# A graph layer with a 32-expert feed-forward on one core: smaller expert blocks, four rounds in place of three, and another way of handing out work beside the edge loop

## The chip, the cores and the metric

The kernel runs on one core of a Trainium2 chip. The metric is the device time of one execution in microseconds, given as the median of several runs; lower is better. Besides the timed runs there is one execution recorded by the hardware profiler, and all durations below come from that one.

## The reference

Only what matters here is kept. There are 6250 nodes with 256 features and 106,250 directed edges (sorted by target) with 64 features each.

```python
xn = layernorm(x)
# 1. edges: gather the source's features, project, SiLU, sum by target, layer norm
msgs = silu(concat(xn[src], edge_attr) @ W + b)            # 106250 x 320 @ 320 x 256
gnn  = layernorm(segment_sum(msgs, dst, 6250)) * gamma + beta
# 2. linear attention: 8 heads of 64, k and v normalised per head
dots = einsum('nhd,nhe->hde', k, v)
attn = einsum('nhd,hde->nhe', q, dots) / 6250 @ Wout.T + bout
x = x + gnn + attn
# 3. top-1 routing to 32 experts, each 256 -> 64 -> 256
xf  = layernorm(x); idx = argmax(xf @ router_w.T + router_b)
h   = relu(xf @ W1[idx] + b1[idx])
out = x + relu(h @ W2[idx] + b2[idx])
```

## The kernel before

Nodes lie in 49 tiles of 128 rows (the last has 106), X holding the running sum and `wide` the transposed normalised rows, later the rows that go to the experts. All arithmetic is f32. The program has three parts.

**The preamble** loads x, normalises it, multiplies it by W's upper part and writes the product to `proj` in DRAM, so that an edge only has to gather a finished 256-row. It also checks that the edges are sorted as assumed (`flag`), and a branch on all engines then takes either `ordered`, the normal path, or `general`, a slow one that works for any edges.

**The edge loop** in `ordered` goes over 208 groups of 512 edges. Per group GpSimd (POOL) issues four indirect gathers of 128 rows (L1213), three groups ahead; TensorE (PE) turns the edge features (`turn`, L1229) and multiplies them (L1356); VectorE (DVE) adds the gathered rows (L1360) and makes a selection matrix (L1366); ScalarE (ACT) applies SiLU (L1377); and every second group PE sums messages by target in two levels (`level1` L1308, `level2` L1335). A gather buffer is free again only after `level1`, so POOL can be at most about three groups ahead of PE. The instruction order is the program's own: the whole of `ordered` is written under a manual schedule, and each engine works through its list in order.

**Everything else** is handed out beside the loop by `Work`: pieces are generators that yield a nominal PE time, DVE time and delay, and `Work.step` runs once per group and takes pieces until an allowance (2.7 us of PE, 3.8 us of DVE, more in one group of two) is spent. The pieces are the attention (`attention_batch`, two tiles at a time, L468 to L503), then for each chunk of tiles whose sums are closed the routing (`chunk`), and then the experts in three rounds of 24, 16 and 9 tiles. A round gives each token a row (`slot`), sends the tokens with indirect writes into the DRAM tensor `xs` (`send`, L854; popped from a list in `gather`, at most two after every second gather), computes expert blocks of 128 rows two at a time (`experts`, `layers`), writes them to `ys`, and reads the results back by token (`collect`, `fetch`, L1024). A block's two weight matrices come from a table in DRAM (`wtab`) that the kernel itself builds (`tabulate`): SyncE (SP) reads the expert's number into a register (L937) and issues one load (L938). The last round is different (`own`): it has one block for each expert, so all weights are loaded in advance by ACT's queue (`own_weights`, after the loop), and the bias is added when the result is read back (L1041 to L1045).

When the loop is over, `Work.drain` runs what is left without an allowance. All 49 read-backs lie there, since `collect` waits for the pool `last` that is opened only then. At the very end a second branch looks at `over`: if a round had too few blocks, the experts are computed again (`again`).

Of the kernel before, what the change touches and what calls it, by code (L numbers as in the profile page):

```python
# [31 lines left out]
CHUNKS = (6, 6, 6, 6, 6, 5, 5, 5, 4)  # L32
CH = max(CHUNKS)
FIRST = (3, 6, 10, 10, 10, 10)
AB = 2
BB = 2
LEAD = 3
AHEAD = 4
BESIDE = 2
ALLOWANCE = (2.7, 3.8)  # L40


ROUNDS = ((24, 44), (16, 38), (9, None))
# [11 lines left out]
def kernel(  # L55
# [167 lines left out]
    counting = const.tile([P, 3, P], BF16, name="counting")  # L223
    nc.vector.tensor_copy(counting[:, 2, :], ident)
# [18 lines left out]
    row_of = const.tile([P, NQ], F32, name="row_of")  # L243
    flag = const.tile([1, 1], I32, name="flag")
# [31 lines left out]
    with tc.tile_pool(name="prep", bufs=2) as prep, tc.tile_pool(name="pre_ps", bufs=2, space=PSUM) as pre_ps:  # L276
# [88 lines left out]
        nc.vector.tensor_copy(flag, pb)  # L365
# [43 lines left out]
    WROW = DC * HID + D  # L409
    wtab = dram.tile([NE, P, WROW], F32, name="wtab")  # L410

    def tabulate(engine, e0, e1):
        q = slice(e0, e1)
        a = DC * HID
        engine.dma_start(
            wtab[q, :, :a].rearrange("e p w -> (e p) w"), w1[q, :, :].rearrange("e (p c) h -> (e p) (c h)", c=DC)
        )
        for i in range(BB):
            engine.dma_start(wtab[q, i * HID : (i + 1) * HID, a:], w2[q, :, :])

# [3 lines left out]
    def weights(pool, bank, w):  # L424
# [3 lines left out]
        w.update(kv_w=kv_w, dots=dots)  # L428
        nf = 2 * F // P
        raw = pool.tile([P, nf, D], F32, tag="kv", name="raw", bufs=2)  # L430
        nc.sync.dma_start(raw, wqkv[F:, :].rearrange("(f p) c -> p f c", p=P))
# [3 lines left out]
        yield 0.0, 0.0, 1  # L435
        for f in range(0, nf, 2):
            pt = bank("t", [P, DC, 2, P], "pt")
            for c in range(DC):
                for i in range(2):
                    nc.tensor.transpose(pt[:, c, i, :], raw[:, f + i, c * P : (c + 1) * P], ident)  # L440
            nc.scalar.copy(kv_w[:, :, f * P : (f + 2) * P], pt.rearrange("p c i e -> p c (i e)"))
            yield 0.5, 0.0, 0
# [15 lines left out]
    def attention_batch(pool, bank, w, t0, t1):  # L458
# [3 lines left out]
        kv = pool.tile([P, AB, 2, F], F32, name="kv", bufs=2)  # L462
        var = small.tile([P, AB * 2 * HEADS], F32, name="var")
        for j in range(m):
            for s in range(2):
                b = bank("kv", [P, F], f"kv{s}")
                for c in range(DC):
                    nc.tensor.matmul(  # L468
                        b, xnT(t0 + j, c), kv_w[:, c, s * F : (s + 1) * F], start=(c == 0), stop=(c == DC - 1)
                    )  # L470
                nc.scalar.copy(kv[:, j, s, :], b)
                yield 1.9, 0.0, 1
            sq = pool.tile([P, 2 * HEADS, DH], F32, name="sq")
            nc.scalar.activation(sq, kv[:, j].rearrange("p s (h d) -> p (s h) d", d=DH), AF.Square)  # L474
# [4 lines left out]
        yield 0.0, 0.0, 1  # L479
# [5 lines left out]
        yield 0.0, 2.4, 1  # L485
        for j in range(m):
            k = kv[:, j, 0, :].rearrange("p (h d) -> p h d", d=DH)
# [3 lines left out]
        for h in range(HP):  # L491
            for j in range(m):
                for i in range(2):
# [3 lines left out]
                        kv[:, j, 0, q],  # L497
                        kv[:, j, 1, q],
# [4 lines left out]
        nc.vector.tensor_add(dots, pd, dots)  # L503
        yield 0.6 * m, 0.4, 0

    def attention_matrix(pool, bank, w):

        raw = pool.tile([P, 2, HP, D], F32, tag="kv", name="raw", bufs=2)
        wq, rawo = raw[:, 0], raw[:, 1].rearrange("p h c -> p (h c)")
# [4 lines left out]
        made = pool.tile([P, 2, HP, D], F32, tag="kv", name="made", bufs=2)  # L514
        qd, wo_t = made[:, 0], made[:, 1]
        diag = pool.tile([P, HP, P], F32, tag="sq", name="diag")
        nc.vector.memset(diag, 0.0)
        yield 0.0, 0.2, 1
# [24 lines left out]
    class Nodes:  # L543


        def __init__(self, pool, bank, rounds, in_order):
# [10 lines left out]
            self.so_far = pool.tile([P, BB, NE], F32, name="so_far")  # L557
# [4 lines left out]
            most = (N + (P - 1) * NE) // P + BB  # L562
            self.number = pool.tile([BB * NE, most], F32, name="number")
# [7 lines left out]

            self.upto = pool.tile([BB * NE, BB * NE], F32, name="upto")
            self.b2_sb = pool.tile([BB * NE, D], F32, name="b2_sb")
            nc.vector.memset(self.upto, 0.0)
            for i in range(BB):
                q = slice(i * NE, (i + 1) * NE)
                nc.vector.tensor_add(self.upto[q, q], after[q, q], ident[q, q])
                nc.sync.dma_start(self.b2_sb[q, :], b2)
# [24 lines left out]
            self.at = {}  # L603

        def clear(self, r, b0, b1):
            nc.sync.dma_start(
                r.xs[b0 * P : b1 * P, :].rearrange("(b p) d -> p b d", p=P),
                zero[:, None, :].to_broadcast([P, b1 - b0, D]),
# [24 lines left out]

        def chunk(self, t0, t1):
# [11 lines left out]
            for t in range(t0, t1):  # L646
                p = self.bank("kv", [P, D], "pres")
                for c in range(DC):
                    nc.tensor.matmul(p, xnT(t, c), mix[:, c, :], start=(c == 0), stop=(c == DC - 1))
                nc.vector.tensor_add(X[:, t, :], p, X[:, t, :])  # L650
                moments(mv2, t - t0, X[:, t, :])
                yield 0.9, 1.0, 0
            self.at[t0] = 1
            yield 0.0, 0.0, 1
# [3 lines left out]
            yield 0.0, 2.2, 1  # L658
# [64 lines left out]
            nc.tensor.matmul(pr[:, 1, 0, :], ones[0:1, :], self.so_far[0:1, 0, :], start=True, stop=True)  # L723
# [9 lines left out]
            nc.vector.tensor_copy(self.so_far, ahead[:, None, :, m].to_broadcast([P, BB, NE]))  # L733
            nc.vector.tensor_mul(logit, logit, hot)
            nc.vector.tensor_reduce(self.rank[:, t0:t1], logit, axis=AX.X, op=ALU.add)
            yield 1.2, 2.2, 1
            self.at[t0] = 3
            if r.own:
                row = small.tile([P, CH], F32, name="place")
                nc.vector.scalar_tensor_tensor(  # L740
                    row[:, :m], top[:, :m], float(-P), self.rank[:, t0:t1], op0=ALU.mult, op1=ALU.add
                )
                nc.vector.tensor_scalar_add(row[:, :m], row[:, :m], float(NE * P))
                self.within(r, t0, t1, row, self.rank[:, t0:t1], P)
                if t1 == r.t1:
                    most = small.tile([1, 1], F32, name="most")
                    nc.vector.tensor_reduce(most, self.so_far[0:1, 0, :], axis=AX.X, op=ALU.max)
                    self.count(most, P)
# [5 lines left out]
        def within(self, r, t0, t1, row, what, limit):  # L754
# [6 lines left out]
                float((r.nb - r.t0) * P),  # L761
# [8 lines left out]
            nc.vector.tensor_scalar_min(self.back[:, t0:t1], self.slot[:, t0:t1], float(r.nb * P - 1))  # L770
# [6 lines left out]
        def places(self, pool, r):  # L777
# [3 lines left out]
            def to_blocks(p, shape, name):  # L781
                i = pool.tile(shape, I32, name=f"{name}_i", bufs=1)
                nc.vector.tensor_scalar_add(i, p, float(P - 1))
                nc.vector.tensor_scalar(i, i, 7, None, op0=ALU.logical_shift_right)
# [4 lines left out]
            both = BB * NE  # L789
            pe = self.bank("kv", [both, 1], "pcount")  # L790
            counts = self.so_far[0:1, :, :].rearrange("o i e -> o (i e)")
            nc.tensor.matmul(pe, counts, ones[0:1, 0:1], start=True, stop=True)
            blocks = to_blocks(self.so_far[:, 0, :], [P, NE], "blocks")
# [4 lines left out]
            column = to_blocks(pe, [both, 1], "column")  # L798
            for c0, c1 in chunks:
                if not t0 <= c0 < t1:  # L800
# [10 lines left out]
                    row[:, :m], first[:, :m], float(P), self.rank[:, c0:c1], op0=ALU.mult, op1=ALU.add  # L811
                )
                self.within(r, c0, c1, row, row[:, :m], nb * P)
# [3 lines left out]
            pe = self.bank("kv", [both, 1], "pends")  # L817
            nc.tensor.matmul(pe, self.upto, column, start=True, stop=True)
            ends = pool.tile([both, 2], F32, name="ends", bufs=1)
# [3 lines left out]
            passed = pool.tile([both, nb], F32, name=f"passed{r.name}", bufs=1)  # L823
            nc.vector.tensor_scalar(passed, number, ends[:, 1:2], None, op0=ALU.is_ge)
            chosen = pool.tile([both, nb], F32, name=f"chosen{r.name}", bufs=1)
# [5 lines left out]
            nc.tensor.matmul(px, ones[:NE, 0:1], passed[:NE, :], start=True, stop=True)  # L831
# [728 lines left out]
    with path.Else():  # L1560
        general()
# [45 lines left out]
```

## Time and profile before

| what | value |
|---|---|
| median of 3 runs | 1425.09 us (1419.56 to 1426.43) |
| profiled execution | 1422.18 us, span 1420.5 us |
| PE, DVE, ACT, POOL busy | 1118.7, 851.6, 541.2, 939.6 us |
| mean granted TensorE clock | 0.877 of full speed |
| DMA | 245.16 MB, mean 173 GB/s |
| first gather issued / last one | 104.0 us / 1217.5 us |

The span is what the profiler recorded from first to last event; the 1.7 us between it and the execution's own time lie around it. Busy times overlap, and idle time of an engine costs nothing unless another waits for it. PE is busy for the largest share, but its share is an average over stages with different limits.

### The profile page before, as it was taken

What the parts mean: (1) busy time and instruction counts of PE and PEld (TensorE: products, weight loads), DVE (VectorE), ACT (ScalarE), POOL (GpSimd) and SP (SyncE); (2) the same over time, 40 slices, a digit from 0 to 9 for tenths busy, and PEclk for the clock granted to TensorE, in tenths of its full rate; (3) what the DMA queues carried; (4) which work ended last, traced back from release to release, by engine and by line L of the source; (5) the groups of instructions that cost most, each with busy time, mean ns of one, the idle gap of its engine ahead of it and who ended that gap; (6) DMA issues with size and microseconds to landing.
All of it is one profiled execution on the core that took longest, in us unless ns stands there. A gap on an engine that the chain in (4) does not pass through costs nothing.

```text
span 1420.5 us, 22703 instructions
## 1 busy us (share of the span) xinstructions
PE 1118.7 (79%) x7340; PEld 656.5 (46%) x7340; DVE 851.6 (60%) x2256; ACT 541.2 (38%) x987; POOL 939.6 (66%) x1050
## 2 busy tenths in 40 slices
PE   4876898899988888988987875489889766857862
PEld 3653444445444444545654543255555433534440
DVE  6933766767766676677876773256556644435342
ACT  2543555455445444543333332134344322212120
POOL 3537777777777777777777777777777677316222
PEclk9997999999999999999999877599999797866585
DMA  7238777655555554445444444478887546589672
GB/s 242 78 107 234 203 198 213 198 172 168 160 156 169 159 170 131 130 131 164 133 127 134 132 119 121 143 203 243 250 241 217 139 118 191 160 244 282 210 242 71
DMA packets 251813, 245.16 MB, mean 173 GB/s; under 512 B 130176, under 2 KB 221736, under 8 KB 251676
## 3 DMA queue, kind: packets, MB, share of 16 engines
q0 software_dynamic: 44960, 121.67, 29.3%
q1 hardware_dynamic: 196152, 113.91, 27.3%
q10 hardware_dynamic: 10564, 7.95, 1.9%
q8 instruction: 63, 1.03, 0.3%
q14 instruction: 74, 0.61, 0.2%
HBM read 194.34 MB, written 55.38 MB: 176 GB/s over the span
## 4 chain that ended last, share of the span: by engine, by line


## 5 line engine op out<-in xcount | busy, mean ns | idle before, releaser
L1213 POOL DMA_INDIRECT gat<-proj,src_T x831 | 796.8, 959 | 266.4 <-issue 219.8
L1360 DVE TENSOR_TENSOR gat<-h,gat 128x1024 f32<-128x1024 f32 x208 | 254.1, 1222 | 280.2 <-PE h L1356 148.0
L1377 ACT ACTIVATE gat<-gat 128x1024 f32<-128x1024 f32 x208 | 219.8, 1057 | 242.9 <-DVE gat L1360 205.8
L1356 PE MATMUL h<-ge,eT 64*128 64x256 f32 x1664 | 251.6, 423 | 33.2 <-DVE gat L1360 32.3
L1356 PEld LDWEIGHTS h<-ge,eT 64*128 64x128 f32 x1664 | 155.0, 198 | 137.1 <-issue 98.8
L1335 PE MATMUL sum<-part,s 128*128 128x256 f32 x400 | 129.6, 452 | 93.3 <-DVE s L1324 93.0
L468 PE MATMUL kv<-kv_w,wide 128*128 128x512 f32 x392 | 188.0, 606 | 3.2 <-DVE kv_w L450 3.2
L1233 ACT COPY eT<-pt 128x256 f32<-128x256 f32 x208 | 77.3, 371 | 204.6 <-PE pt L1229 195.0
L1335 PEld LDWEIGHTS sum<-part,s 128*128 128x128 f32 x400 | 78.7, 215 | 144.8 <-DVE s L1324 129.0
L1308 PE MATMUL po<-gat,s 128*32 128x256 f32 x1664 | 130.8, 439 | 0.0
L1024 POOL DMA_INDIRECT ot<-yso,back x49 | 48.5, 990 | 101.3 <-DVE wide L688 28.0
L1317 ACT COPY part<-po 128x256 f32<-128x256 f32 x104 | 38.7, 372 | 187.2 <-PE po L1308 187.2
L1229 PE MATMUL pt<-ident,ea 128*128 128x128 f32 x416 | 93.7, 308 | 2.2 <-DMA ea<-in_edge_attr_dram 1.4
L468 PEld LDWEIGHTS kv<-kv_w,wide 128*128 128x128 f32 x392 | 68.4, 193 | 57.5 <-issue 52.3
L475 DVE TENSOR_REDUCE var<-sq 128x16 f32<-128x1024 f32 x49 | 59.7, 1218 | 52.1 <-ACT sq L474 52.0
L896 DVE COPY xbT<-pt 128x512 f32<-128x512 f32 x57 | 39.2, 688 | 73.9 <-PE pt L894 73.7
L1308 PEld LDWEIGHTS po<-gat,s 128*32 128x32 f32 x1664 | 47.8, 121 | 67.7 <-issue 35.8
L1229 PEld LDWEIGHTS pt<-ident,ea 128*128 128x128 f32 x416 | 42.8, 144 | 75.2 <-issue 50.0
L854 POOL DMA_INDIRECT xso<-wide,slot x49 | 49.3, 1006 | 27.1 <-DVE back L770 16.7
L299 POOL TENSOR_TENSOR X<-X,bo 128x256 f32<-128x256 f32 x49 | 35.5, 746 | 47.7 <-ACT xn L296 25.9
L894 PE MATMUL pt<-ident,xb 128*128 128x128 f32 x228 | 49.2, 349 | 21.6 <-DMA xb<-xso 19.9
L306 PE MATMUL pp<-gw,wide 128*128 128x256 f32 (+1 forms) x196 | 53.5, 417 | 13.8 <-ACT wide L303 6.6
(264 smaller groups left out, 1391.7 us busy)
## 6 DMA issues: line engine op xcount, KB each, us to landing
ea<-in_edge_attr_dram SPq DMA_DIRECT2D x207, 128.0 KB
xb<-xso SPq DMA_DIRECT2D x57, 256.0 KB
xso<-zero SPq DMA_DIRECT2D x28, 512.0 KB
wt<-wtab SPq DMA_DIRECT2D x72, 192.0 KB
gat<-proj,src_T POOLq DMA_INDIRECT x831
yso<-xb SPq DMA_DIRECT2D x41, 256.0 KB
wtab<-in_L_ffn_W_dram SPq DMA_DIRECT2D x24, 256.0 KB
out_dram<-ot SPq DMA_DIRECT2D x48, 128.0 KB
```

The costliest lines, as they stand in the source:

```text
L306: nc.tensor.matmul(pp[:n, :], xnT(t, c, n), gw[:, c, :], start=(c == 0), stop=(c == DC - 1))
L468: nc.tensor.matmul(b, xnT(t0 + j, c), kv_w[:, c, s * F : (s + 1) * F], start=(c == 0), stop=(c == DC - 1))
L475: nc.vector.tensor_reduce(var[:, j * 2 * HEADS : (j + 1) * 2 * HEADS], sq, axis=AX.X, op=ALU.add)
L854: ins = nc.gpsimd.indirect_dma_start(out=r.xs[:], out_offset=bass.IndirectOffsetOnAxis(ap=self.slot[:n, t : t + 1], axis=0), in_=wide[:n, ...
L1213: nc.gpsimd.indirect_dma_start(out=gat[:n, k % 2, k // 2, :], out_offset=None, in_=proj[:], in_offset=bass.IndirectOffsetOnAxis(ap=src_T[: ...
L1229: nc.tensor.transpose(pt[:, j, :], ea[:, 2 * j : 2 * j + 2, :].rearrange("p k d -> p (k d)"), ident)
L1233: nc.scalar.copy(eT, pt)
L1308: nc.tensor.matmul(po[k * wide_k : (k + 1) * wide_k, :], s1[:, k, :], msg[:, k % 2, k // 2, :], start=(g == here[0]), stop=(g == here[-1]) ...
L1335: nc.tensor.matmul(sums[t], s2[:, (t - lo) * P : (t - lo + 1) * P], part, start=(q == opens[t]), stop=(q == closes[t]),)
L1356: nc.tensor.matmul(h[:, s, j, :], eTs[g][half, j, :], ge[half, :], start=True, stop=True)
L1360: nc.vector.tensor_add(gats[g], h, gats[g])
L1377: nc.scalar.activation(gats[g], gats[g], AF.Silu)
```

## The change

Six things change together.

1. Expert blocks have 64 rows (HB) and are computed four at a time, a "quad" of 256 rows, where before there were pairs of 128. In `layers` the bias product comes first, and each half of an output tile belongs to another expert.
2. The rounds are 28, 11, 5 and 5 tiles; the last two are `own` rounds with one 64-row block per expert. The last chunks are 3 and 2 tiles.
3. The table `wtab` is gone. A quad loads W1 and W2 of its four experts straight from the inputs (eight loads, four register reads). The `own` weights go into the places of `wide` whose tokens have been sent, during the loop, on SP's queue; read-backs use places of `wide` too. The own rounds add their bias on PE, as the others do.
4. `Work.step` runs twice a group, before and after SiLU and the sums, with half the allowance each, and up to 1.5 us not spent is carried over. Attention may have three batches in flight in place of two, with smaller buffers; the products with `mix` of later tiles are made as soon as `mix` is known.
5. The last groups' sums are written out behind the loop, which has 208 iterations in place of 212; the last chunks are urgent.
6. The branch at the start and `again` are gone: `ordered` always runs, and one branch at the end runs `general` if either check failed.

```diff
-CHUNKS = (6, 6, 6, 6, 6, 5, 5, 5, 4)
+CHUNKS = (6, 6, 5, 5, 6, 6, 5, 5, 3, 2)
+HB = 64
+QB = 2 * BB
-ALLOWANCE = (2.7, 3.8)
-ROUNDS = ((24, 44), (16, 38), (9, None))
+ALLOWANCE = (((1.9, 2.0), (1.9, 2.0)), ((1.3, 1.8), (0.3, 1.8)))
+CARRY = 1.5
+ROUNDS = ((28, 76), (11, 44), (5, None), (5, None))
+BACK = (32, 44)
...
+            for j in pairs:
+                for i in range(BB):
+                    nc.tensor.matmul(py[j][i * HB : (i + 1) * HB, :], one_of(BB * j + i).to_broadcast([NE, HB]),
+                        self.b2_sb, start=True, stop=False, tile_position=(0, i * HB))
+            for j in pairs:
+                for i in range(BB):
+                    half = slice(i * HID, (i + 1) * HID)
+                    nc.tensor.matmul(py[j][i * HB : (i + 1) * HB, :], hid[half, j, :], w2_of(BB * j + i, half),
+                        start=False, stop=True, tile_position=(i * HID, i * HB))
...
         def experts(self, pool, r, b0):
-                last = queue.dma_start(w[:, i, :], wtab[bass.ds(e, 1), :, :].rearrange("o p w -> p (o w)"))
+                queue.dma_start(wa[:, b : b + 1, :], w1[bass.ds(e, 1), :, :].rearrange("o (p c) h -> p o (c h)", c=DC))
+                last = queue.dma_start(wb[i * HID : (i + 1) * HID, j : j + 1, :], w2[bass.ds(e, 1), :, :].rearrange("o h d -> h o d"))
...
+        def own_weights(self):
+            for q in range(NE // QB):
+                e = slice(QB * q, QB * (q + 1))
+                while not all(self.work.turn >= self.gone.get(t, 1 << 30) + 6 for t in range(QB * q, QB * (q + 1))):
+                    yield 0.0, 0.0, 1
+                nc.sync.dma_start(wide[:, QB * q : QB * q + 2, :]..., w1[e, :, :]...)
+                nc.sync.dma_start(wide[:, QB * q + 2 : QB * (q + 1), :], w2[e, :, :]...)
+                self.weights_in += 1
+                yield 0.0, 0.0, 4
...
         def collect(self, r, t0, t1):
+                    at = BACK[0] + self.returns % (BACK[1] - BACK[0])
+                    ot = wide[:, at, :]
...
-                    nc.vector.tensor_add(ot[:n, :], ot[:n, :], X[:n, t, :])
+                nc.vector.tensor_add(X[:n, t, :], ot[:n, :], X[:n, t, :])
-                nc.sync.dma_start(out[t * P : t * P + n, :], ot[:n, :])
+            move_rows(nc.sync, X[:, t0:t1, :], t0, t1, out, True)
...
-            self.left = [min(left, 0.0) + more for left, more in zip(self.left, allowance)]
+            self.left = [min(left, CARRY) + more for left, more in zip(self.left, allowance)]
...
-                if g < NG:
-                    nc.scalar.activation(gats[g], gats[g], AF.Silu)
-                work.step([a + (s if summing else -s) for a, s in zip(ALLOWANCE, (-1.1, -0.2))])
+                work.step(ALLOWANCE[summing][0])
+                nc.scalar.activation(gats[g], gats[g], AF.Silu)
...
+                work.step(ALLOWANCE[summing][1])
...
-            with tc.tile_pool(name="last", bufs=2, side="right") as nodes.last:
-                nodes.own_weights(nodes.last)
-                work.drain()
+            work.drain()
...
-    unlike = nc.values_load(flag[0:1, 0:1], min_val=0, max_val=1 << 20)
-    with tc.If(unlike < 1) as path:
...
+    with ExitStack() as arm:
+        with tc.manual_schedule():
+            ordered(arm)
+    wrong = nc.values_load(flag[0:1, 0:1], min_val=0, max_val=1 << 20)
+    with tc.If(wrong > 0):
         general()
```

## The prediction

> **What bounds the kernel now.** I read the page's busy shares first, then the costliest groups, the work by stage, the waits, and last the timeline of the end.
>
> ```profile
> PE 1118.7 (79%) x7340; PEld 656.5 (46%) x7340; DVE 851.6 (60%) x2256; ACT 541.2 (38%) x987; POOL 939.6 (66%) x1050
> ...
> L1213 POOL DMA_INDIRECT gat<-proj,src_T x831 | 796.8, 959 | 266.4 <-issue 219.8
> ```
>
> PE has the largest share, but POOL's gathers set the loop. Their idle time is "issue": 678 gaps of 0.3 us that nothing else ends. A gather thus costs 1.25 us, a group of four 5.0 us. The stages (columns: busy us and count of PE, PEld, DVE, ACT, POOL; granted clock; DMA share; GB/s) say the same:
>
> ```profile
> 300.00:400.00 100.00, 93.30 (x670) 49.07 (x670) 70.82 (x170) 52.12 (x84) 75.92 (x80) 1.00 0.58 168
> ...
> 1000.00:1100.00 100.00, 87.83 (x663) 53.72 (x662) 55.22 (x124) 42.45 (x90) 72.36 (x77) 0.98 0.80 236
> ```
>
> 80 gathers in 100 us is exactly one per 1.25 us, with PE 93% busy. Only where experts run densely (77) does POOL slip. From the first gather at 104 to the last one's end at 1218.4 there are 831 gathers (1039 us) and 40 sends at 1.28 us (51 us), so stalls are only 24 of 1114 us. The other 202 us of the span lie behind the last gather:
>
> ```profile
> 1217.50 0.89 POOL L1213 DMA_INDIRECT gat<-proj,src_T  x1 [0.30 <-issue]
> ...
> 1244.75 0.70 PE L1335 MATMUL sum<-part,s 128*128 128x256 f32 x2
> ...
> 1263.44 0.37 ACT L911 ACTIVATE hid<-phid,b_colo 128x128 f32<-128x128 f32 x1 [16.04 <-DMA w_own<-in_L_ffn_W_dram]
> ...
> 1332.90 1.12 PE L902 MATMUL phid<-xbT,w_own 128*64 128x128 f32 x8 [0.79 <-DVE xbT L896]
> ...
> 1381.11 0.70 PE L923 MATMUL py<-w_own,hid 64*128 64x256 f32 x4 [0.55 <-ACT hid L911]
> ...
> 1402.44 0.13 DVE L1555 CAST lacking<-over 1x1 int32<-1x1 f32 x1
> ```
>
> The last sum comes 26 us after the last gather; ACT stands 16 us behind the loads of the own weights; sixteen own pairs take 48.9 us; 20.7 us later the last tile is added; and 18 us pass until the end. So there are two budgets: a loop bound by POOL, and a tail of chained steps.
>
> **Part 1: the start.** The branch at the start costs almost nothing: POOL's first instruction behind it waits for the last preamble work (row_of) until 102.4. In the changed order it still waits for all engines and queues. Bounds 0 to -1.5 us; I take -0.5: first gather at 103.5.
>
> **Part 2: the loop.** POOL's list keeps 831 gathers; 44 sends in place of 40 lie among them: +4 x 1.28 = +5 us. Unstalled, the last gather would end at 103.5 + 1039 + 56 = 1198. Now the stalls.
>
> PE: I counted the matmuls between two groups in both orders and multiplied by full-clock start-to-start times of the timeline: four h 1.07, an ea turn 0.14, a kv product 0.905, sixteen pdot 1.08, a sum 0.53, eight po 1.0. A quad: four turns 0.56, hidden 0.65, bias 1.07, second layer 1.07 (four half-height matmuls cost what four h cost), 3.4 us; a pair takes 2.8. Nominal allowances average 2.7 us a group as before, yet more gets done, because 33 quads are inside the loop against some 25 pairs: 897 us of PE in the loop against 841. Per group, in groups 8 to 96 (attention) it goes from 4.4 to 4.8 us; in 144 to 168 (round 0's quads) from 3.7 to 5.1; in 184 to 200 from 3.4 to 4.8. POOL's 5.0 still covers the means, but hardly any slack is left, and stretches of eight groups reach 5.2 to 5.4. A gather three groups ahead (15 us) absorbs such a stretch; light ones (2.4 to 3.2 in 112 to 128) let PE catch up. DVE, counted likewise, stays under 5.0 except in 96 to 104 (5.3); ACT is far below.
>
> SP: a block costs one register read and one load, a quad four reads and eight loads.
>
> ```profile
> 1043.13 0.46 SPq L873 DMA_DIRECT2D xb<-xso  x1
> 1044.66 1.85 SPq L938 DMA_DIRECT2D wt<-wtab  x2
> 1046.62 0.39 SPq L1198 DMA_DIRECT2D ea<-in_edge_attr_dram  x1
> ```
>
> From `xb` to the next line is 3.5 us for two blocks, some of it slow issue; usual values are 0.75 for a read and 0.41 for an issue. A quad: 4 x 0.75 + 8 x 0.41 + 0.45 + 0.38 = 7.1 us, against 3.2 for a pair. In the 24 groups with 17 quads SP needs 17 x 7.1 + 24 x 0.42 for `ea` + some clears = 135 us, POOL 120. That is 15 us too many, just the lead. Behind a late quad stand the edge loads on SP and the next h on PE. `own_weights` adds 16 loads to SP's list in the loop that wait for sends; they are handed out six half-group turns after the send, about when POOL gets there, so I give them no time (0 to 5 us). Without the table (24 loads of 256 KB) and with fewer padded rows (11,776 for 14,592, each cleared, loaded and stored) some 15 MB are moved less, which speaks against contention.
>
> I take 38 us of stalls in place of 24 (bounds 15, if smoother handing out helps, and 80): the last gather ends at L = 1236, 18 us later than now. Attention and the first 30 quads are complete by then.
>
> **Part 3: the tail.** Times are after L, in the changed order. Last h at +5, gather add, SiLU, part and last sum: +14 (now +26, behind expert work). DVE closes the two last tiles: statistics 2.2, inverse root 2.4, +19. The routing of the 3-tile chunk alternates on PE and DVE with own quads of round 2, 3.4 us each: its places are known at about +41. POOL meanwhile makes 12 read-backs (+15), idles until +41, makes 3 sends and 13 read-backs (+61), then the two last sends (+64); the last places (about +58) are ready. SP's read of `flag` waits for them too, with round 3's loads behind it, but those need the sends anyway. On DVE 36 adds stand ahead of the first `xbT` of round 3; the 36th read-back is 11 after the sends, +78, landed at +80. Hence round 3 starts at +80, though its rows could be there at about +69. Its eight quads cost 3.4 us at full clock; own pairs took 48.9/16 = 3.06 against 2.11 in their best stretch (1346.57 to 1350.80), a factor 1.45, so 5.0 each: +120. From the last product to the last add are 20.7 us now with nine read-backs; five are 4 x 1.25 us fewer: +136. The 18 us of the end stay (one skip in place of two; the nearest row is the end itself, bounds 12 to 22): +154. The 16 us behind the own weights are gone, being loaded in the loop.
>
> The sum: 1236 + 154 = 1390 us of span against 1420.5. With the 1.7 us around it 1392, against 1422.2 for the profiled execution: -2.1%. That execution is 0.2% below the median of 1425.09, so I leave it at 1392.
>
> **Two rules that speak against it.** Each output tile of the second layer now gets two half-height products, from different rows of the array, in one PSUM bank; before each had its own. In this trace four `po` products share a bank (1.0 us for eight) but use column tiles only. The Trainium skill, page "TensorEngine Tiling (Array Packing)", section "Gotcha 1: PSUM Pressure", says that different row tiles cannot access the same bank at a time. By the row a quad's second layer is 1.07, by the rule 2.13. The two tiles write different partitions, as po's do, so I take the row; the rule would give +15 us in the loop and +15 in the tail.
>
> The granted clock in 1300:1325 was 0.50, in 1350:1375 0.81. The page "TensorE: Matmul & The Clock Gate", Part 1, has only half and full clock, chosen by how busy PE just was; a tail with gaps would stay at half, 6.8 us a quad and +14 us. I keep the measured factor 1.45.
>
> **The rivals.** (a) Forecast, 0.50: 1360 to 1420. (b) Smoother loop and full clock, 0.20: stalls 15, tail 141: 1213 + 141 + 2 = 1356. For it: half-size turns, and PE idles of about 1 us at `sum` that the new order fills. Against: PE at 96% in the attention stage. (c) The bank rule, 0.12: 1392 + 30 = 1422, no change. (d) SP's queue becomes the bound, 0.18: if loads queue up and a quad costs 10 us, groups 144 to 168 take 49 us too long after the lead is used up, round 1's eleven quads 17 more; L is 1236 - 12 + 66 = 1290 and the end 1446, slower. It decides from about 9 us a quad. For it: the own-weight loads on ACT's queue took up to 3.8 us each to issue at a DMA share of 0.97. Against: 0.36 us is the usual issue even at 0.80. (e) That the last branch runs `general` would double the time. From the reference's own inputs the rounds need 70 of 76 and 38 of 44 blocks, and at most 51 and 45 of 64 rows: excluded.
>
> **The numbers.** A run can tell about 0.5%, 7 us, from no change. Faster by more: nearly all of (a), (b), some of (c): 0.72; within: 0.09; slower: (d) and part of (c), 0.19. The range, 1350 to 1445, takes in (b) and (c) and (d) up to its price.
>
> **What would show it.** Right: the last gather ends at 1225 to 1255; POOL idles some 25 us after its first 12 read-backs; the first `xbT` of the last round waits behind adds; own quads at 4 to 6 us; no wait for own weights. Wrong: POOL's rate well under 80 in 100 us in the attention stage (PE is the bound), edge loads late behind weight loads (d), a second layer of 2 us at full clock (c), or an L near 1215 (b).

## The result: 14% slower, with all of it lost inside the edge loop

| | before | after |
|---|---|---|
| median | 1425.24 us (1419.56 to 1426.43) | 1626.63 us (1624.24 to 1627.99) |
| profiled execution, span | 1422.18, 1420.5 us | 1627.99, 1625.7 us |
| loop: first gather to end of the last | 104.0 to 1218.4 = 1114 us | 105.5 to 1477.2 = 1372 us |
| behind the last gather | 202 us | 148.5 us |
| mean granted clock | 0.877 | 0.834 |

The ratio is 1.142, with a 95% interval of 1.139 to 1.145. The forecast was 1392. The tail is within 6 us of its forecast of 154; the loop, forecast at 1236 less 103.5, or 1132 us, is 240 us too long. Against before, the loop lost 258 us and the tail won 54.

Four rows of the page of after, and behind them two of before. The group rows give busy us and mean ns, then the idle time of the engine ahead of the instruction and what ended most of it.

```profile
PE 1206.1 (74%) x7897; PEld 700.9 (43%) x7897; DVE 846.7 (52%) x2264; ACT 551.4 (34%) x1013; POOL 939.4 (58%) x1050
...
L1203 POOL DMA_INDIRECT gat<-proj,src_T x831 | 795.9, 958 | 518.8 <-issue 443.2
L1345 DVE TENSOR_TENSOR gat<-h,gat 128x1024 f32<-128x1024 f32 x208 | 254.3, 1223 | 409.6 <-PE h L1343 262.6
...
L1323 PE MATMUL sum<-part,s 128*128 128x256 f32 x400 | 143.5, 491 | 142.1 <-DVE s L1312 141.3
```

```profile
L1360 DVE TENSOR_TENSOR gat<-h,gat 128x1024 f32<-128x1024 f32 x208 | 254.1, 1222 | 280.2 <-PE h L1356 148.0
...
L1335 PE MATMUL sum<-part,s 128*128 128x256 f32 x400 | 129.6, 452 | 93.3 <-DVE s L1324 93.0
```

The busy times of POOL and DVE are those of before within 1%, and PE has 8% more. The shares of all engines have fallen, so none of them is the bound over the whole span. What has grown is waiting: POOL's idle time ahead of gathers from 266 to 519 us, DVE's for `h` from 148 to 263, PE's at the sums from 93 to 142. The work by stage (busy us and count of PE, PEld, DVE, ACT, POOL; granted clock; DMA share; GB/s) shows where:

```profile
300.00:400.00 100.00, 82.21 (x543) 43.47 (x543) 59.74 (x137) 42.26 (x65) 60.55 (x63) 0.91 0.43 119
...
1100.00:1200.00 100.00, 80.91 (x622) 47.26 (x622) 40.96 (x95) 32.17 (x73) 46.39 (x50) 0.81 0.64 182
```

There are 63 gathers in 100 us in the attention stage, where there were 80 and where no quad exists yet, and 50 in a stretch dense with quads. PE did less in 100 us than before (82 for 93), so it waits too. The timeline of the attention stage shows for what:

```profile
318.23 2.08 PE L1323 MATMUL sum<-part,s 128*128 128x256 f32 x4 [4.45 <-DVE s L1312]
...
322.91 1.23 DVE L1345 TENSOR_TENSOR gat<-h,gat 128x1024 f32<-128x1024 f32 x1 [1.33 <-PE h L1343]
...
324.24 5.42 PE L470 MATMUL kv<-kv_w,wide 128*128 128x512 f32 x12
...
328.46 1.06 ACT L1362 ACTIVATE gat<-gat 128x1024 f32<-128x1024 f32 x1
...
329.59 1.13 PE L1343 MATMUL h<-ge,eT 64*128 64x256 f32 x8
...
330.77 1.23 DVE L1345 TENSOR_TENSOR gat<-h,gat 128x1024 f32<-128x1024 f32 x1 [5.99 <-PE h L1343]
```

PE stands 4.45 us until DVE has made the selection matrix; from 324.24 on it makes three kv products at one go (four records each, 5.4 us), and DVE stands 6.0 us, because the next `h` comes behind them. SiLU of the gather add that ended at 324.1 starts at 328.5, behind two kv copies. First one engine waits and then the other; before, most groups had one kv product (69 of the 88 counted below).

### The profile page after: what moved, and what is told of

Same layout as the page of the kernel before. It is cut to its first block, busy times and chain, and to the rows that moved or that the text cites. A ratio compares the mean times of both kernels' runs of the same rounds, so it can differ in the third digit from the quotient of the medians.

```text
span 1625.7 us, 24247 instructions
## 1 busy us (share of the span) xinstructions
PE 1206.1 (74%) x7897; PEld 700.9 (43%) x7897; DVE 846.7 (52%) x2264; ACT 551.4 (34%) x1013; POOL 939.4 (58%) x1050
## 3 DMA queue, kind: packets, MB, share of 16 engines
q8 instruction: 66, 1.08, 0.3%
## 5 line engine op out<-in xcount | busy, mean ns | idle before, releaser
L1345 DVE TENSOR_TENSOR gat<-h,gat 128x1024 f32<-128x1024 f32 x208 | 254.3, 1223 | 409.6 <-PE h L1343 262.6
L1343 PE MATMUL h<-ge,eT 64*128 64x256 f32 x1664 | 268.3, 446 | 59.0 <-DVE gat L1345 43.7
L1323 PE MATMUL sum<-part,s 128*128 128x256 f32 x400 | 143.5, 491 | 142.1 <-DVE s L1312 141.3
L1343 PEld LDWEIGHTS h<-ge,eT 64*128 64x128 f32 x1664 | 163.5, 210 | 164.3 <-issue 87.0
L1323 PEld LDWEIGHTS sum<-part,s 128*128 128x128 f32 x400 | 85.0, 234 | 183.0 <-DVE s L1312 167.0
L1296 PE MATMUL po<-gat,s 128*32 128x256 f32 x1664 | 141.0, 468 | 0.0
L473 ACT COPY kv<-kv 128x512 f32<-128x512 f32 x98 | 56.8, 582 | 114.3 <-PE kv L470 114.3
L916 DVE COPY xbT<-pt 128x512 f32<-128x512 f32 x46 | 31.7, 689 | 120.1 <-PE pt L914 120.1
L914 PE MATMUL pt<-ident,xb 128*128 128x128 f32 x184 | 40.2, 353 | 71.9 <-DMA xb<-xso 70.3
L1040 POOL DMA_INDIRECT wide<-yso,back x49 | 48.8, 997 | 42.8 <-DMA yso<-xb 28.2
L964 ACT ACTIVATE xb<-py 128x256 f32<-128x256 f32 x92 | 34.6, 383 | 102.6 <-PE py L955 93.7
```

The lines of the kernel that those rows point to most:

```text
L473: nc.scalar.copy(kv[j][:, s, :], b)
L914: nc.tensor.transpose(pt[:, j, c, :], feats[:, c, :], ident)
L1040: nc.gpsimd.indirect_dma_start(out=ot[:n, :], out_offset=None, in_=r.ys[:], in_offset=bass.IndirectOffsetOnAxis(ap=self.back[:n, t : t + 1 ...
L1296: nc.tensor.matmul(po[k * wide_k : (k + 1) * wide_k, :], s1[:, k, :], msg[:, k % 2, k // 2, :], start=(g == here[0]), stop=(g == here[-1]) ...
L1323: nc.tensor.matmul(sums[t], s2[:, (t - lo) * P : (t - lo + 1) * P], part, start=(q == opens[t]), stop=(q == closes[t]),)
L1343: nc.tensor.matmul(h[:, s, j, :], eTs[g][half, j, :], ge[half, :], start=True, stop=True)
```

## The experiments

The theories at the start were these. **A**: what a step leaves unspent is carried over (CARRY), and lumps come from that. **B**: the two steps stand in the wrong place, above all the first one ahead of SiLU. **C**: delays are counted in turns, a turn is now half a group, and attention has three batches in flight, so that dependent work is issued right behind what it waits for. Against them stood quads and SP's queue, the prediction's own rival (d).

**E1, nothing carried.**

```diff
-CARRY = 1.5
+CARRY = 0.0
```

> The changed kernel (1626.6 us) with CARRY = 0: what a step leaves unspent is lost, as before the change. Theory A (the carried allowance lets several kv products into one place, so that PE, ACT and DVE take turns waiting): the attention stage comes back to 75 to 80 gathers in 100 us, 1480 to 1530 us in all. Theory B (the place of SiLU behind the first step) and theory C (attention's shorter delays): less than 30 us of change, 1600 to 1640 us.

1577.7 us: 49 faster. In this order the carry is part of the loss and not most of it.

**E2, SiLU ahead of both steps.**

```diff
-                work.step(ALLOWANCE[summing][0])
                 nc.scalar.activation(gats[g], gats[g], AF.Silu)
+                work.step(ALLOWANCE[summing][0])
```

> The changed kernel with SiLU issued ahead of the first of the two steps, nothing else. Theory B (SiLU stands on ScalarE behind kv copies that wait for PE, and level1, the gather buffers and POOL wait for SiLU): 75 to 80 gathers in 100 us in the attention stage and the same relief beside the experts, 1450 to 1520 us. Theories A and C: 1600 to 1630 us; the wait of the first step's work on PE stays.

1648.9 us: 22 slower, the opposite of theory B. Work ahead of SiLU is not what costs (E14 below says so too). In the order, the move puts all kv copies behind SiLU, which itself waits for the gather add; that this is the reason was not shown.

**E3, one step a group.** The step comes behind SiLU and ahead of the sums, with the sum of the allowances, nothing carried, delays halved.

```diff
-                work.step(ALLOWANCE[summing][0])
                 nc.scalar.activation(gats[g], gats[g], AF.Silu)
+                work.step(ALLOWANCE[summing])
...
-                work.step(ALLOWANCE[summing][1])
...
-            piece.due = self.turn + delay
+            piece.due = self.turn + (delay + 1) // 2
```

> The changed kernel with work handed out as before the change: one step a group, behind SiLU and ahead of the sums, the two allowances added up, nothing carried over, delays halved because a turn is a whole group again. Attention keeps its three batches in flight, experts their quads. If handing out (A or B) is the cause, the loop comes back to nearly the predicted length: 1400 to 1450 us. Theory C (three batches with short delays): 1560 to 1630. If SP's queue or the quads are the cause beside the experts, the attention stage recovers (75 to 80 gathers in 100 us) and the expert stages do not (about 55): about 1500.

1496.1 us: 131 of the 201 us are back. The total is the one expected of SP's queue or quads, but the stages are the other way round. The attention stage has only 65 to 72 gathers in 100 us, hardly more than E1 (60 to 69): the first 480 gathers, by which all kv products are made, take 694 us (before 608, after 747). The rest of the loop takes 524 us (before 507, after 624), at 57, 72 and 63 gathers in 100 us between 1000 and 1300, and with 21 of the 46 quads in it where after has 32. The waits of the attention stage between 200 and 600 (total us, number, longest):

```profile
PE h L1343 <- ACT eT L1223: 46.3, 10, 6.8
...
ACT sq L476 <- DVE var L478: 51.6, 11, 6.7
```

ScalarE stands at a square, whose single buffer is held until VectorE has reduced the one before; `eT` is behind it, and `h` behind `eT`. That fits C. Before has a single buffer too, but issues the reduction right behind the square, where after issues it a turn later.

**E4, attention's order of before**, two steps and carry kept: two batches in flight, before's delays in whole groups, and the reduction right behind its square.

```diff
-                yield 1.9, 0.0, s
+                yield 1.9, 0.0, 2
             sq = pool.tile(...)
             nc.scalar.activation(sq, ...)
-            yield 0.0, 0.0, 1
...
+        yield 0.0, 0.0, 2
...
-                    while batches[-3:-2] and not batches[-3].done:
+                    while batches[-2:-1] and not batches[-2].done:
```

> The changed kernel with attention's order as before: two batches in flight, and the delays of before in whole groups (twice the number of half-group turns), two steps and carry kept. Theory C (a product's copy, square and reduction are issued right behind each other, so every engine waits for the other): the attention stage recovers to 75 to 80 gathers in 100 us, 1480 to 1530 us. Theories A and B: 1590 to 1640 us.

1563.8 us: 63 faster. There are 69 to 73 gathers in 100 us in the attention stage, and still 50 to 60 beside the experts. The edit takes back several things at once; which of them counts was not separated.

**E5, one step and attention's order of before together** (E3's and E4's edits, of which these are the core).

```diff
-CARRY = 1.5
+CARRY = 0.0
...
+                work.step(ALLOWANCE[summing])
...
-                yield 1.9, 0.0, s
+                yield 1.9, 0.0, 2
```

> One step a group, nothing carried, attention's order of before, a third time, for a chip on which the kernel before takes its 1425 us. 1400 to 1430 us if the loss lies in how work is laid beside the loop alone; 1440 to 1480 us if quads or SP's queue hold the loop beside the experts. On a chip where the kernel before takes 1859 us: the same as before within 1%.

1414.7 us, ratio to before 0.9935 (0.991 to 0.996). The whole loss is gone, with quads, direct weight loads and four rounds in place. The stages of this kernel, and its gathers (min, median, max ns; first and last start):

```profile
300.00:400.00 100.00, 93.04 (x653) 48.41 (x650) 69.58 (x155) 53.22 (x84) 75.93 (x80) 1.00 0.54 148
...
900.00:1000.00 100.00, 56.14 (x362) 34.61 (x360) 38.35 (x97) 23.42 (x41) 75.58 (x103) 0.73 0.47 140
1000.00:1100.00 100.00, 84.54 (x665) 49.06 (x666) 47.12 (x110) 37.42 (x81) 67.36 (x73) 0.86 0.79 223
...
L1203 POOL DMA_INDIRECT gat<-proj,src_T x831: 887/946/2294, 105.8 to 1233.6; - x167
```

The attention stage has 80 gathers in 100 us again, and the last one starts at 1233.6, about where the prediction had it (1236). Between 1000 and 1100 eight quads begin (counted by their `xbT`), beside 73 gathers; in after, seven beside 53, and nine beside 50 in the next 100 us. E15 below has eight beside 81. So quads and SP's eight loads each do not by themselves hold the loop. But the match with 1236 means less than it seems: only 19 quads lie in this loop, where 33 were forecast and after has 32. The other 27 make the tail 176 us long, for 154 forecast.

**E6, a second buffer of squares in E3.** Four kv buffers in place of five make room.

```diff
-KV = 5
+KV = 4
...
-            sq = pool.tile([P, 2 * HEADS, DH], F32, name="sq")
+            sq = pool.tile([P, 2 * HEADS, DH], F32, name="sq", bufs=2)
```

> The kernel of 1496 us (one step, nothing carried, attention's three batches kept) with a second buffer for the squares and four kv buffers in place of five to make room. Theory: what is left of the attention stage's loss there is ScalarE standing at a square until VectorE has reduced the one before (51.6 us between 200 and 600, with eT and the next h behind it); with two buffers that wait goes and the stage comes to 73 to 80 gathers in 100 us, 1430 to 1460 us. Rival (three batches with short delays lay products, copies and reductions too close whatever the buffers): 1480 to 1505 us.

Inconclusive: 1842.5 us, on a chip on which the kernel before took 1858.8 itself. E5, E7 and E8 were also first run there, E5 and E7 twice; every order tried there came to between 1839 and 1874 us, which tells nothing. E6 was not repeated, so how much of E3's rest is the single buffer, and how much the three batches, stays open. E5, E7 and E8 were repeated on a chip where before takes 1423 to 1428; those runs are told here.

**E7, the kernel before with the changed handing-out alone**: two steps, halved allowances, carry, every delay doubled in the loop.

```diff
+                work.step(ALLOWANCE[summing][0])
                 if g < NG:
                     nc.scalar.activation(gats[g], gats[g], AF.Silu)
-                work.step([a + (s if summing else -s) for a, s in zip(ALLOWANCE, (-1.1, -0.2))])
...
+                work.step(ALLOWANCE[summing][1])
...
-            self.left = [min(left, 0.0) + more for ...]
+            self.left = [min(left, CARRY) + more for ...]
-            piece.due = self.turn + delay
+            piece.due = self.turn + delay * (1 if self.draining else 2)
```

> The kernel before with the changed handing-out alone: two steps a group, 1.5 us carried, delays twice as many half-group turns. Theory (handing out in half groups costs by itself, with pairs of 128 rows too): about as much as between 1415 and 1520 us in the changed kernel, so 1490 to 1540 us. Rival (it costs only with quads): 1415 to 1450 us.

1411.7 us, 0.989 of before (0.983 to 0.995): faster by 1%, where the two expectations had it slower, or 1415 at best. With before's attention and pairs, two steps and a carry cost nothing.

**E8, the kernel before with the changed attention alone**, one step a group. The functions for attention are those of after.

```diff
+KV = 5
...
-        kv = pool.tile([P, AB, 2, F], F32, name="kv", bufs=2)
+            kv.append(pool.tile([P, 2, F], F32, name="kv", bufs=KV))
...
-                yield 1.9, 0.0, 1
+                yield 1.9, 0.0, s
...
-                    while batches[-2:-1] and not batches[-2].done:
+                    while batches[-3:-2] and not batches[-3].done:
```

> The kernel before with the changed attention alone (three batches in flight, both products of a tile behind one another, the reduction of the squares a turn later), one step a group. Theory: it costs what undoing it brought in the one-step kernel, 1496 less 1415 or 80 us: 1480 to 1520 us. By the count of the order, where the sum over the groups of the longest of PE, DVE and POOL is 1149 us against 1103, at least 45 us. Rival: 1415 to 1445 us.

1523.7 us: 96 slower. C costs by itself, with pairs and one step; its attention stage makes 63 to 68 gathers in 100 us, and behind it the loop takes what it took before (504 us for 507).

**E9, E4 with longer delays.** A delay of one turn becomes two, so that quads too get a whole group between their stages.

```diff
-            piece.due = self.turn + delay
+            piece.due = self.turn + (2 if delay == 1 and not self.draining else delay)
```

> The changed kernel with two steps and carry kept, attention's order as before, and in addition every delay of one turn made two in the loop, so that a step of a quad follows the one before it a whole group later, as it did before the change. Theory C widened (with turns of half a group the products, copies and activations of a quad stand right behind each other, and each engine waits for the other): the stages beside the experts go from 50 to 58 up to 70 or more gathers in 100 us, 1440 to 1490 us. Rival (two steps or the carry themselves cost it): as with attention's order alone, 1550 to 1570 us.

1520.2 us: 44 faster than E4, between the two expectations. The stretch dense with quads makes 59 gathers, not 70. All of the gain lies behind the attention stage (47 us); the first 480 gathers take 680 us for E4's 673.

**E11, E5 with the carry of 1.5 us; E12, E4 with nothing carried.** The one line of each, E11's first:

```diff
-CARRY = 0.0
+CARRY = 1.5
```

```diff
-CARRY = 1.5
+CARRY = 0.0
```

> The kernel of 1415 us (one step, attention's order of before) with the carry of 1.5 us put back. Theory A for the rest (the carry makes lumps; the sum over the groups of the longest engine rises from 1116 to 1154 us): 1440 to 1470 us. Rival (two half steps are the rest, the carry only moves work from the tail into the loop): 1395 to 1420 us.

> The changed kernel with attention's order of before (1564 us) and nothing carried, two steps kept. Theory A (the carry): 1420 to 1460 us. Rival (two steps, because of where the second one stands, right ahead of the next h): 1510 to 1560 us.

E11 takes 1452.5 us, 38 more than E5; E12 takes 1510.2, 54 less than E4 and 96 more than E5. So there are both a price of the carry and a price of two steps, though E7 pays neither. Beside the experts the carry is not a cost of order alone: it brings ten more quads out of the tail into the loop (29 for 19), and the loop behind the 480th gather takes 585 us for 519, the tail 148 for 176. Of the 96 us between E12 and E5, 29 lie in the first 480 gathers and 91 behind them, less 20 in the tail. E12 has the quads' delays of half a group, which E9 took out of E4 for 47 us. E7 has doubled delays and brings only one pair more into the loop (26 for 25); that fits its paying nothing there (505 us).

For the attention stage, what is different in E7 is seen in the order. I counted where the 49 squares stand on ScalarE: between `eT` and SiLU (first step), between SiLU and the next `eT` or `part` (second step of a group without sums), or behind `part` (second step of a group with sums). E7 has 48, 1 and 0; E12 has 14, 19 and 16; E9 has 9, 3 and 37. The waits of VectorE between 200 and 600 for a square, first in E9 and then in E7:

```profile
DVE var L477 <- ACT sq L476: 63.3, 25, 4.3
```

```profile
DVE var L476 <- ACT sq L475: 0.3, 2, 0.2
```

Behind the sums, a square stands on ScalarE behind `part`, which waits for `po` on PE; its reduction stands on VectorE right ahead of the next gather add. E14 tries whether this place is what costs.

**E14, E9 with every piece that has waited due in the first step** (an odd turn is a first step). It takes E4 and a rounding in place of E9's delay.

```diff
-            piece.due = self.turn + delay
+            piece.due = self.turn + delay + ((self.turn + delay + 1) % 2 if delay and not self.draining else 0)
```

> The changed kernel with two steps, the carry of 1.5 us and attention's order of before, and every piece that has waited due only in the first step of a group (behind eT, ahead of SiLU): all 49 squares stand there, 90 of 98 kv copies. Theory (the place: what is issued behind the sums stands on ScalarE behind part, which waits for po, and on VectorE right ahead of the next gather add): the attention stage comes to 77 to 80 gathers in 100 us, and with the carry's dense experts as in the one-step kernel with carry (1452 us) 1430 to 1475 us in all. Rival (two steps with quads cost it wherever the work stands): 1500 to 1530 us.

1455.5 us: 65 faster than E9, within 3 us of E11, which has one step and the same carry. All 49 squares and 90 of 98 kv copies stand in the first step; the attention stage:

```profile
300.00:400.00 100.00, 91.70 (x654) 47.72 (x648) 68.41 (x159) 51.85 (x81) 75.93 (x80) 1.00 0.56 149
```

The first 480 gathers take 609 us for E9's 680; the loop behind them is unchanged (587 us for 588). It is the place that decides in the attention stage: with its work ahead of SiLU two steps cost what one step costs. The rounding also makes some waits longer, but E9's longer delays left this stage where E4 had it. What is left of the loss lies beside the experts (61 gathers between 1000 and 1100), as in E11.

**E15, E5 with other rounds.**

```diff
-ROUNDS = ((28, 76), (11, 44), (5, None), (5, None))
+ROUNDS = ((22, 64), (17, 56), (5, None), (5, None))
```

> The version of 1415 us (one step, nothing carried, attention's order of before) with rounds of 22, 17, 5 and 5 tiles in place of 28, 11, 5 and 5 (64 and 56 blocks for 76 and 44, of which 58 and 51 are needed): the first expert round starts six tiles earlier, in the stretch of 900 to 1000 us where PE is only 56% busy and POOL has nothing but gathers. The same number of quads, some two more of them in the loop, so the tail is shorter by two quads of 4 to 5 us: 1400 to 1412 us, if the stretch takes them for nothing; 1415 to 1430 if they make groups longer as elsewhere.

1389.1 us, 0.976 of before (0.973 to 0.979), which is faster than both kernels. It is 11 us below the lower end of what was expected. The loop took the earlier quads for nothing (22 lie in it, three more than in E5), and the tail shrank by more than two quads: the last gather is issued at 1229.4 (E5: 1233.6), and 157 us follow it (E5: 176). Part of that is probably the sends: in E5 and E3 ten of the 49 come behind the last gather, in E15 and in E1, E2, E4, E9, E11, E12 and E14 five, and only E5 and E3 have tails of 169 us or more. No run tests it alone.

```profile
900.00:1000.00 100.00, 73.66 (x528) 44.99 (x532) 45.07 (x104) 30.59 (x62) 74.16 (x89) 0.83 0.69 195
1000.00:1100.00 100.00, 84.19 (x712) 50.27 (x706) 56.41 (x142) 39.33 (x84) 75.36 (x81) 0.91 0.78 226
```

PE is busy for 74 us between 900 and 1000 in place of 56, and the next stretch makes 81 gathers where E5 made 73. POOL did not have "nothing but gathers" in E5's first stretch, as was expected: 28 of its instructions there are sends, beside 47 gathers.

**The ladder.** The edits stack up in this order (another order would share them out otherwise, as E1 and E3 show). The last four columns are read from the traces: us from the start of the first gather to that of the 481st; from there to the end of the last gather; what lies behind; and the quads that begin in the loop (before: pairs).

| kernel | us | gain | first 480 gathers | rest of loop | tail | quads in loop |
|---|---|---|---|---|---|---|
| before | 1425.2 | | 608 | 507 | 202 | 25 of 57 |
| after | 1626.6 | | 747 | 624 | 149 | 32 of 46 |
| attention's order of before (E4) | 1563.8 | 63 | 673 | 635 | 149 | 32 |
| delays of one turn made two (E9) | 1520.2 | 44 | 680 | 588 | 146 | 28 |
| waiting work into the first step (E14) | 1455.5 | 65 | 609 | 587 | 149 | 30 |
| one step and nothing carried (E5) | 1414.7 | 41 | 610 | 519 | 176 | 19 |
| rounds of 22, 17, 5, 5 (E15) | 1389.1 | 26 | 609 | 516 | 157 | 22 |

After lost 140 us in the attention stage, which E4 and E14 bring back, and 118 beside the experts, of which E9 brings back 47. The rest comes back in E5, but with eleven quads fewer in the loop. Whether the carry costs there by making lumps, or by the quads that it brings in, was not separated.

## Why the prediction was wrong

**Part 1, the start: right in size.** The first gather is at 105.5, not 103.5.

**Part 2, the loop: the step that failed.** The loop's gathers and sends are 1095 us, as counted (831 x 1.25 and 44 x 1.28). The term that was mis-sized is the stalls: 38 us taken, at most 80, and 277 measured (1372 less 1095). The sentence that led there is "POOL's 5.0 still covers the means". Means over eight groups are the wrong sum. With one `h` buffer, PE and DVE meet in every group, and a long group on PE is not made good by a short one when DVE's long group comes next. Taking the same counted durations, but adding up for each group the longest of PE, DVE and POOL's 5.0, gives 1103 us before (measured 1114) and 1196 after; these are counts from the order, not measurements (a recount from the order in the traces gives 1096 and 1179). In groups 8 to 96 the means of PE and DVE are 4.75 and 4.40, and the mean of the longest is 6.06; before it was 5.39. There the groups with 0, 1, 2 and 3 kv products number 11, 69, 8 and 0 before, and 30, 30, 24 and 4 after. So the order that I had in hand would have shown some 93 us of the loss.

The other 176 us between that sum and the measured loop (before, 11) lie inside the groups, in chains of waits from engine to engine. The runs show what they come with: attention's changed order (E4, E8), delays of half a group (E9) and work placed behind the sums (E14), and beside the experts the carry with the quads that it brings in (E11). How the 176 us split over single waits was not shown. I read "two steps" and "three batches" as a smoother handing-out, and took the shorter delays for nothing. I named no work that would cover a square's wait for a reduction, and there was none.

**PE's load: right, and not what mattered.** "PE at 96% in the attention stage" and "hardly any slack is left" pointed at one of the stages that lost, for the wrong reason: PE is 82% busy there after.

**SP's queue (rival d): not the main cause.** A quad took 7.8 and 8.15 us on SP (from one `xb` load to the next: 1116.79, 1124.58, 1132.73), more than the 7.1 worked out and under the 9 from which it would decide. All waits of PE for edge loads in after come to 5.4 us, and E5 runs the same loads in a loop of 1129 us. What was left out is the token rows: in after's loop PE waits 44 us for `xb` and 13 for W1 (E5: 27 and 3; before: 20 for `xb`). So some of the 118 us lost beside the experts may hang on the loads; no run tests that.

**Own weights in the loop: right.** No wait for them is among those of the tail.

**The bank rule: the row was right.** Four half-height products into two banks, with different row and column tiles, took as long as the bias products, at a granted clock of 1.00 (1130 to 1136):

```profile
1132.49 1.08 PE L944 MATMUL py<-b_sb,choseno 32*64 32x256 f32 x8
...
1133.50 1.08 PE L955 MATMUL py<-w2t,hid 64*64 64x256 f32 x8
```

Taken as one row tile after the other, the rule in the section "Gotcha 1: PSUM Pressure" of the Trainium skill's page "TensorEngine Tiling (Array Packing)" would have made the second row about 2.1 us (an estimate: twice 1.07). For two row tiles that write different partitions of a bank, the row does not show that.

**Part 3, the tail: 148.5 us for 154, with errors that cancel.**

```profile
1491.44 0.95 POOL L1040 DMA_INDIRECT wide<-yso,back  x1 [0.30 <-issue]
...
1528.21 1.13 POOL L872 DMA_INDIRECT xso<-wide,slot  x1 [35.68 <-DVE back L790]
...
1569.82 0.68 DVE L916 COPY xbT<-pt 128x512 f32<-128x512 f32 x1
...
1574.57 1.97 PE L955 MATMUL py<-wide,hid 64*64 64x256 f32 x8
...
1579.17 1.08 PE L955 MATMUL py<-wide,hid 64*64 64x256 f32 x8
...
1590.65 1.08 PE L955 MATMUL py<-wide,hid 64*64 64x256 f32 x8
...
1593.97 1.08 PE L955 MATMUL py<-wide,hid 64*64 64x256 f32 x8
...
1605.12 0.94 POOL L1040 DMA_INDIRECT wide<-yso,back  x1 [28.15 <-DMA yso<-xb]
```

After twelve read-backs POOL idles 36 us (25 were forecast), so the sends come at +51 (L, the end of the last gather, is 1477.2) and the last round's first `xbT`, behind the adds on DVE as forecast, at +93 in place of +80. Its eight quads then take 30 us (1570.6 to 1601.0), 3.8 each where I had taken 5.0, and the last ones follow each other every 3.3 us (1590.65 to 1593.97), the forecast's full-clock price of 3.4. The end behind the last add is 9 us, not 18. The granted clock was 0.50 from 1550 to 1575, with PE busy for 5.5 us, and 0.95 from 1575 to 1600, with PE busy for 23.6; the second-layer products took 1.97 us at 1574.57 and 1.08 from 1579.17 on. That fits the half and full clock of the Trainium skill's page "TensorE: Matmul & The Clock Gate", Part 1. The fear that the tail would stay at half did not come true, and the factor of 1.45 that I carried over from before was wrong as well.

**What would make it wrong.** The forecast named "POOL's rate well under 80 in 100 us in the attention stage" as the sign, and it came; but it put "PE is the bound" in brackets behind it, and that was not the cause. None of the rivals was a loss by order, with every engine busy for a smaller share than before.

## What to carry to other kernels

When engines meet every iteration over a single buffer, add up the longest engine of each iteration, not the mean of each engine, before believing that a reordering is free; here that sum is a lower bound, and shows 93 of the 258 us. A delay counted in steps shrinks when steps become smaller; recount every delay as the time that its wait takes. Split a difference by stage before giving it a cause, and count what work lies in each stage: E5's short loop holds thirteen quads fewer than after's. When all engines' shares fall together and the loop gets longer, look for work issued right behind what it waits for, and for work placed behind an instruction that waits; moving it to another point of the same iteration brought 65 us here.

## What the runs showed of the hardware that I had not expected

One chip ran the kernel before in 1858.8 us (1833 to 1884, 63 runs), and on it five orders with quite different loops agreed within 2%, among them E8, which elsewhere is 7% slower than before. In the trace of E7 there, a gather's median is 949 ns and a gather add's 1225, as elsewhere (946 and 1223), yet POOL makes 60 gathers in 100 us. The granted clock is lower (0.79, for 0.88 in E7 elsewhere), and the median of a `po` record is 634 ns for 379. Longer, too, are waits that end with nothing recorded ("remote"); between 200 and 700, in us, number and longest:

```profile
DVE gat L1361 <- remote: 58.8, 16, 8.6
...
ACT eT L1234 <- remote: 49.8, 16, 5.4
```

`eT` waits only for TensorE. In that stretch 19 of these copies start 0.5 to 5.4 us later than both the recorded end of their turn and the end of ScalarE's instruction before; in the kernel before, elsewhere, none is later by more than 0.1. The ends of TensorE's instructions are modelled in these traces, so either its results arrive late there or the ends are given too early. Which it is, and why this chip is slower, stays open.
